# First and last turns of a graph-attention pipeline listed step by step, weights loaded in 21 transfers

## The chip, the core and the metric

The kernel runs on one core of a Trainium2 chip. A core has five engines with queues of their own: TensorE (matrix products, results into PSUM), VectorE, ScalarE, GpSimd and SyncE, which here only issues DMAs. Each engine works through its own queue in order and waits on semaphores for the others; 16 DMA engines move the data. The metric is the device time in microseconds of one execution; several executions give a median.

## The reference

There are 64 graphs of 256 nodes with 512 features, and two layers. All of it is float32.

```python
# layer 0, per graph
deg = sum(adj, -1);  agg = adj @ x / max(deg, 1e-6)
x = layernorm(x + relu(concat([x, agg], 2) @ W.T))
# layer 1, per graph: 8 heads of 64
q, k, v = x @ Wq.T + bq, x @ Wk.T + bk, x @ Wv.T + bv
scores = (q @ k.T) * 64 ** -0.5 * (adj + adj)
ctx = softmax(scores) @ v
out = layernorm(x + ctx @ Wo.T + bo)
```

## The kernel before

One graph goes through a chain of steps. A step is a small function, kept in a table by its name and called with a graph's number; the instructions it issues go into the queues of whatever engines they need. The names:

- `Dzx`, `Dza`, `Dx`, `Dadj` load x and the adjacency from HBM on SyncE's queue, in four DMAs each (`Dzx`, `Dza` in an order that VectorE's 32x32 block transposes `xT0`, `xT1`, `aT` turn into transposed tiles). `deg` makes the reciprocal degrees.
- `L1` to `L7` are layer 0's weight products, `AY0`, `AY1` the neighbour sums, `AYa`, `AYb`, `AYp`, `AYn` the joining, the statistics (VectorE), factors (GpSimd) and application (ScalarE) of the first norm, for each half of the rows.
- `Dway` stores the normalized rows to HBM, `Dz1` loads them in the order for the transpose `x1T`, and `Drest` loads them again for the residual, to which `bo` adds the bias row on GpSimd (line 496).
- `Q1` to `Q7` are the q and k projections together, `V1` to `V7` the v projection.
- `Sa` to `Sd` are the scores of four pairs of heads, and for each pair: `m` the mask and `M` the negated maximum (VectorE), `e` and `f` the exponentials (ScalarE), `r` the reciprocal, `n` the scaling (ScalarE), `T` a block transpose (VectorE), `Dw` a store to HBM and `Ds` its load as the transposed matrix.
- `C0a`, `C0b`, `C1a`, `C1b` are the context products, `c0`, `c1` ScalarE's copies of them out of PSUM, `O1` to `O7` the output projection, `lb`, `lp`, `ln` the last norm, `Dout` the store.

Each of the four projections (L, Q, V, O) is one level of a Strassen-Winograd scheme: seven products of half-size blocks in place of eight (line 307). The products need sums of blocks of the weights (`T1` to `T4`, made once) and of the tokens (`xS1` to `xS4`, `yS`, `cS`, on GpSimd, line 288). Products that share a PSUM bank accumulate in it; between them a bank's content is taken out by a `k` step (`Lk1`: a copy) or a `j` step (`Lj3`: an addition to what is there), so that `L6`, say, waits for `Lk1`.

The order of the work is written out by hand: `PLAN` is one turn of a software pipeline, and `name+n` means that in turn i the step is run for graph i+n. The loop at the end runs turns from -6 to B+5; a step for a graph that doesn't exist, or one already run, is left out. The same text thus serves the first and last turns.

The weights are loaded ahead of the turns, by `first_weights` and `more_loads`: a block at a time, and, except for wo, in four groups of 32 partitions, so 16 DMAs of 64 KB for each 512 x 512 matrix (w0 has two of these), 4 for wo. W0's lower half, wq and the four bias loads go on ScalarE's queue, the others on SyncE's. Tiles have a slot per block sum; T3 starts as the loaded block B12, which `sum_blocks` overwrites. `later_weights` (scalings and sums of wq and wk on VectorE, of wv on GpSimd) and `last_weights` (bv times wo into the bias row, sums of wo) run in the middle of the turns where graph 0 gets to `V2` and to `bo`.

Of the kernel before, what the change touches and what calls it, by code (L numbers as in the profile page):

```python
# [18 lines left out]

PLAN = """  # L20
# [37 lines left out]
    Q2+1 Qk4+1 AYp1+2 ln1-1 Qj2+1  # L58
"""
# [3 lines left out]
def kernel(  # L63
# [88 lines left out]
    B11, B21, B22, T1, T2, T3, T4 = range(7)  # L152
    w0 = const.tile([P, 7, 2, 2, G], F32, name="w0")
    wqk = const.tile([P, 7, 2, 2, G], F32, name="wqk")
    wv = const.tile([P, 7, 2, G], F32, name="wv")
    wo = const.tile([P, 7, 2, G], F32, name="wo")

    def load_blocks(queue, dst, dram, swapped=False, natural=False):

        for blk, kh, nh in ((B11, 0, 0), (T3, 0, 1), (B21, 1, 0), (B22, 1, 1)):  # L160
            nh ^= swapped
            cols = dram[:, nh * G : (nh + 1) * G]
            if natural:
                rows = cols.rearrange("(c p) o -> p c o", p=P)
                queue.dma_start(out=dst(slice(None), blk), in_=rows[:, 2 * kh : 2 * kh + 2])
                continue
            rows = cols.rearrange("(a c l) o -> a l c o", a=A, c=FC)
            for a, part in groups():
                queue.dma_start(out=dst(part, blk), in_=rows[a, :, 2 * kh : 2 * kh + 2])

    def sum_blocks(engine, w):
        for dst, a, b in ((T1, T3, B11), (T2, B22, T1), (T3, B22, T3), (T4, B21, T2)):
            engine.tensor_tensor(w[:, dst], w[:, a], w[:, b], ALU.subtract)  # L173

# [4 lines left out]
    def first_weights():  # L179
        load_blocks(nc.scalar, lambda p, k: w0[p, k, :, 1], w0t[F:])  # L180
        load_blocks(nc.sync, lambda p, k: w0[p, k, :, 0], w0t[:F])
        load_blocks(nc.scalar, lambda p, k: wqk[p, k, :, 0], wqt, swapped=True)
        nc.scalar.dma_start(out=bqk[:, 0], in_=bq)
        nc.scalar.dma_start(out=bqk[:, 1], in_=bk)
        nc.scalar.dma_start(out=bvT, in_=bv.rearrange("o (c p) -> p (o c)", p=P))
        nc.scalar.dma_start(out=bo_sb, in_=bo.to_broadcast([P, F]))
        for name in ("xT0", "xT1", "xS1", "xS2", "xS4", "xS3"):
            run(name, 0)
        sum_blocks(nc.vector, w0.rearrange("p k c m o -> p k (c m o)"))

    def more_loads():
        load_blocks(nc.sync, lambda p, k: wqk[p, k, :, 1], wkt, swapped=True)
        load_blocks(nc.sync, lambda p, k: wv[p, k], wvt)
        load_blocks(nc.sync, lambda p, k: wo[p, k], wot, natural=True)

    def later_weights():
        nc.vector.tensor_scalar(bqk[:, 0], bqk[:, 0], QSCALE, None, ALU.mult)
        for k in (B11, T3, B21, B22):
            nc.vector.tensor_scalar(wqk[:, k, :, 0], wqk[:, k, :, 0], QSCALE, None, ALU.mult)
        sum_blocks(nc.vector, wqk.rearrange("p k c m o -> p k (c m o)"))  # L200
        sum_blocks(nc.gpsimd, wv.rearrange("p k c o -> p k (c o)"))

    def last_weights():

        bv_all = tile_of("bv_all", 0, [P, NT, F], tag="h1")[:, 0].rearrange("p (c q) -> p c q", c=FC)
        nc.vector.tensor_copy(bv_all, bvT.unsqueeze(2).to_broadcast([P, FC, P]))
        ps = bank("p_bv", 0)
        for n, blocks in enumerate(((B11, B21), (T3, B22))):
            for c in range(FC):
                nc.tensor.matmul(  # L210
                    ps[:, n * G : (n + 1) * G],
                    lhsT=bv_all[:, c],
                    rhs=wo[:, blocks[c // 2], c % 2],
                    start=(c == 0),
                    stop=(c == FC - 1),
                )
        nc.vector.tensor_tensor(bo_sb, ps, bo_sb, ALU.add)
        sum_blocks(nc.gpsimd, wo.rearrange("p k c o -> p k (c o)"))
# [125 lines left out]
    def right_weights(left, w, width):  # L344
        def multiply(k, b, ps, first):
            for c in range(2):
                nc.tensor.matmul(  # L347
                    ps[:, :width],
                    lhsT=left(k, b, c),
                    rhs=w[:, WEIGHTS[k], c],  # L350
# [19 lines left out]
    def multiply_q(k, b, ps, first):  # L370
        for m in range(2):
            for j in range(2):
                for c in range(2):
                    nc.tensor.matmul(  # L374
                        ps.rearrange("p (m j q) -> p m j q", m=2, j=2)[:, m, j],
                        lhsT=wqk[:, WEIGHTS[k], c, m, j * P : (j + 1) * P],
# [264 lines left out]

    plan = [(name[:-2], int(name[-2:])) for name in PLAN.split()]
    done = set()

    def run(name, b):
        if 0 <= b < B and (name, b) not in done:
            done.add((name, b))
            steps[name](b)

    with tc.manual_schedule():  # L650
        run("Dzx", 0)
        first_weights()
        run("Dza", 0)
        run("Dadj", 0)
        run("Dx", 0)
        run("Dadj", 1)
        run("Dadj", 2)
        run("Dzx", 1)
        more_loads()
        for i in range(-6, B + 6):  # L660
            for name, ahead in plan:
                if name == "V2" and i + ahead == 0:
                    later_weights()
                if name == "bo" and i + ahead == 0:
                    last_weights()
                run(name, i + ahead)
# [36 lines left out]
```

## Time and profile before

| | |
|---|---|
| median of 3 runs | 3129.31 us (3128.94 to 3130.68) |
| profiled execution, its own time | 3130.71 us |
| its span, first to last instruction | 3128.9 us |
| TensorE busy | 3062.6 us, 98% of the span |
| VectorE, ScalarE, GpSimd busy | 67%, 55%, 31% |
| DMA | 513.35 MB, 164 GB/s on average |
| mean granted clock of TensorE | 0.992 |

The rows of a timeline read: start, duration (us), engine, line and operation, tiles out<-in, shapes, count, and in brackets how long the engine had been idle and what released it. PE is TensorE's matmuls, PEld its weight loads, DVE VectorE, ACT ScalarE, POOL GpSimd, SPq and ACTq the DMA issues of SyncE and ScalarE. A float32 product shows twice the matmuls that the code has[...]. A count such as "x4" merges equal neighbours.

### The profile page before, as it was taken

The page shows a single profiled execution, that of the slowest core. Times are in us where ns is not written, and L with a number is a line of the kernel's source. Part 1 is how long each engine was busy: PE and PEld are TensorE (multiplying, and loading weights), DVE is VectorE, ACT ScalarE, POOL GpSimd, SP SyncE. Part 2 cuts the span into 40 slices and gives each one's busy share as a digit, 9 for nine tenths or more (in the row PEclk, how much of TensorE's full clock was granted, in tenths as well). Part 3 has the DMA queues.
Part 4 walks back from the last instruction along what each step waited for, and adds up shares of the span by engine and source line. Part 5 has one row for each costly group of instructions (what it writes and reads, how often), then busy time and mean ns, then how long its engine had stood idle before and what let it go on. Part 6 is the DMA issues. An engine that isn't in the chain of part 4 may idle for free. (4 is left out here: it accounts for less than half of the span.)

```text
span 3128.9 us, 51253 instructions
## 1 busy us (share of the span) xinstructions
PE 3062.6 (98%) x17168; PEld 2265.9 (72%) x17168; DVE 2082.1 (67%) x3599; ACT 1712.2 (55%) x4993; POOL 974.2 (31%) x1677
## 2 busy tenths in 40 slices
PE   5999999999999999999999999999999999999996
PEld 2776777777777777777767777777777777777674
DVE  4666666666766766666666666667667666666664
ACT  1555556555555555555555565555555555555654
POOL 2233323323233233233333233232332332333332
PEclk8999999999999999999999999999999999999998
DMA  6565655656656656656666567566566566566555
GB/s 148 125 165 159 182 160 157 185 154 160 182 156 161 182 153 171 173 151 182 165 159 182 154 163 186 155 159 181 157 161 182 152 172 173 151 182 165 159 155 141
DMA packets 498183, 513.35 MB, mean 164 GB/s; under 512 B 114816, under 2 KB 399488, under 8 KB 497920
## 3 DMA queue, kind: packets, MB, share of 16 engines
q1 hardware_dynamic: 494400, 507.70, 60.5%
q8 instruction: 137, 2.24, 0.3%
q10 hardware_dynamic: 3520, 2.37, 0.3%
q14 instruction: 126, 1.03, 0.1%
HBM read 308.55 MB, written 201.33 MB: 163 GB/s over the span
## 5 line engine op out<-in xcount | busy, mean ns | idle before, releaser
L390 ACT ACTIVATE qk<-Qa,bqk 128x128 f32<-128x128 f32 x768 | 218.6, 367 | 241.2 <-PE Qa L374 241.2
L363 ACT COPY oy<-La 128x512 f32<-128x512 f32 x192 | 112.3, 585 | 433.2 <-PE La L347 433.1
L428 POOL TENSOR_SCALAR mv<-mv 128x1 f32<-128x1 f32 x256 | 55.7, 217 | 935.1 <-DVE mv L423 919.4
L405 ACT COPY v<-Va 128x256 f32<-128x256 f32 x192 | 70.1, 365 | 365.3 <-PE Va L347 365.3
L347 PE MATMUL Lc<-w,xS 128*128 128x512 f32 x512 | 249.8, 611 | 14.5 <-DVE w L173 14.5
L374 PEld LDWEIGHTS Qa<-x1T,wqk 128*128 128x128 f32 x2048 | 248.8, 192 | 6.6
L374 PEld LDWEIGHTS Qa<-yS,wqk 128*128 128x128 f32 x2048 | 248.8, 192 | 6.6
L288 POOL TENSOR_TENSOR cS<-cT 128x256 f32<-128x256 f32 x128 | 93.2, 729 | 509.2 <-ACT cT L616 509.2
L374 PE MATMUL Qc<-yS,wqk 128*128 128x128 f32 x2048 | 249.6, 275 | 0.0
L374 PE MATMUL Qa<-x1T,wqk 128*128 128x128 f32 x2048 | 249.3, 275 | 0.0
L374 PE MATMUL Qa<-yS,wqk 128*128 128x128 f32 x2048 | 249.3, 275 | 0.0
L347 PE MATMUL La<-w,xS 128*128 128x512 f32 x512 | 243.3, 598 | 5.4 <-POOL xS L288 3.0
L347 PE MATMUL La<-w,xT 128*128 128x512 f32 x512 | 241.6, 594 | 0.8 <-DVE oy L328 0.8
L374 PEld LDWEIGHTS Qc<-yS,wqk 128*128 128x128 f32 x2048 | 239.0, 192 | 0.0
L442 PE MATMUL AY<-oy,aT 128*128 128x512 f32 x512 | 233.0, 598 | 4.6 <-DVE oy L328 4.6
L415 DVE TENSOR_TENSOR h<-Oa,rest 128x256 f32<-128x256 f32 x192 | 81.5, 425 | 220.3 <-PE Oa L347 200.7
L328 DVE TENSOR_TENSOR oy<-Lc,oy 128x512 f32<-128x512 f32 x64 | 44.2, 691 | 276.0 <-PE Lc L347 271.0
L288 POOL TENSOR_TENSOR yS<-x1T 128x256 f32<-128x256 f32 x128 | 93.3, 729 | 350.2 <-DVE x1T L482 350.2
L347 PEld LDWEIGHTS Lc<-w,xS 128*128 128x128 f32 x512 | 93.2, 192 | 132.3 <-issue 108.8
L288 POOL TENSOR_TENSOR xS<-xT 128x256 f32<-128x256 f32 x128 | 93.4, 730 | 299.1 <-DVE xT L253 299.1
L454 DVE SCALAR_TENSOR_TENSOR oy<-AY,deg,oy 128x512 f32<-128x512 f32 x128 | 94.9, 741 | 135.7 <-PE AY L442 135.7
L546 ACT ACTIVATE sa<-sa,nmaxa 128x256 f32<-128x256 f32 x256 | 127.0, 497 | 99.8 <-DVE nmaxa L540 99.8
(119 smaller groups left out, 7274.4 us busy)
## 6 DMA issues: line engine op xcount, KB each, us to landing
zx<-in_x_dram SPq DMA_DIRECT2D x256, 128.0 KB, 3.6
x<-in_x_dram SPq DMA_DIRECT2D x256, 128.0 KB, 3.4
way<-x SPq DMA_DIRECT2D x64, 512.0 KB, 3.2
z<-way SPq DMA_DIRECT2D x256, 128.0 KB, 3.0
wsa<-sa SPq DMA_DIRECT2D x64, 512.0 KB, 2.6
wsb<-sb SPq DMA_DIRECT2D x64, 512.0 KB, 3.0
sTa<-wsa SPq DMA_DIRECT2D x256, 128.0 KB, 3.6
wsc<-sc SPq DMA_DIRECT2D x64, 512.0 KB, 2.7
```

The source lines that it names most:

```text
L288: nc.gpsimd.tensor_tensor(part_of(s, b, [P, 4, 2, P])[:, k], left(b), right(b), op)
L328: nc.vector.tensor_tensor(dst, ps.rearrange(shape, **sizes), dst, ALU.add)
L347: nc.tensor.matmul(ps[:, :width], lhsT=left(k, b, c), rhs=w[:, WEIGHTS[k], c], start=first and c == 0, stop=True, skip_group_check=True,)
L363: nc.scalar.copy(part_l(b, t, n), ps.rearrange("p (m o) -> p m o", m=2))
L374: nc.tensor.matmul(ps.rearrange("p (m j q) -> p m j q", m=2, j=2)[:, m, j], lhsT=wqk[:, WEIGHTS[k], c, m, j * P : (j + 1) * P], rhs=left_y ...
L390: nc.scalar.activation(part_q(b, t, n)[:, m, j], ps.rearrange("p (m j q) -> p m j q", m=2, j=2)[:, m, j], AF.Identity, bias=bqk[:, m, c : ...
L405: nc.scalar.copy(part_v(b, t, n), ps[:, :G])
L415: nc.vector.tensor_tensor(part_o(b, t, n), ps[:, :G], rest, ALU.add)
L428: nc.gpsimd.tensor_scalar(mv[:, 1:2], mv[:, 1:2], LN_EPS, None, ALU.add)
L442: nc.tensor.matmul(ps, lhsT=held["aT", b][:, j, t], rhs=held["oy", b][:, 1, j], start=(j == 0), stop=(j == NT - 1),)
L454: nc.vector.scalar_tensor_tensor(h, held[f"AY{t}", b], rdeg, h, ALU.mult, ALU.add)
L546: nc.scalar.activation(rows(b)[:, r], rows(b)[:, r], AF.Exp, bias=of("nmax", b)[:, r : r + 1], accum_out=of("total", b)[:, r : r + 1],)
```

## The change

Two texts are added beside `PLAN`: `START` lists, step by step with the graph's number, everything that belongs to the turns before turn 3, and `END` everything from turn 60 on (there `name:n` means graph B-n). The loop runs turns 3 to 59 with `PLAN`, which is as it was. The loads, scalings and sums of weights are steps of their own and stand in `START`: `W0`, `Wq`, `Wv`, `Wo`, `Wb` (loads), `WqS` (scaling of wq and bq), `W0s1` to `Wos4` (sums), `bv1` to `bv3` (the bias row).

A matrix is loaded with its rows whole, in 4 DMAs of 256 KB (wo: one of 1 MB), into a tile whose blocks are views; the sums T1, T2 and T4 have a tile of their own, and T3 overwrites the view of the block B12, as before it overwrote that block's slot. In `W0`, the lower half goes on ScalarE's queue and the upper on SyncE's; all other weights and the biases go on SyncE's. The scaling of wq and bq is on ScalarE, in two instructions; the sums of w0 and wq are on VectorE, those of wv and wo on GpSimd. The right operand of L's products is now two runs of 256 columns, one from each half of w0, where it was 512 columns in a row.

```diff
+FIRST_TURN = 3
+LAST_TURNS = 4
+START = """
+    Dzx:0 W0:0 xT1:0 xT0:0 xS1:0 xS3:0 Dx:0 xS2:0 Dza:0 xS4:0 Dadj:0 Dzx:1 L1:0 W0s1:0 W0s2:0 Dadj:1
+    L2:0 Lk1:0 W0s3:0 Wo:0 L6:0 W0s4:0 deg:0 L5:0 Lk6:0 aT:0 Wb:0 L7:0 Lk5:0 L3:0 Lj7:0 Dza:1 L4:0 Wq:0
+    Lj3:0 Lj2:0 Lk4:0 xT1:1 AY1:0 xT0:1 xS1:1 AY0:0 xS3:1 AYa1:0 L5:1 AYb1:0 AYa0:0 AYp1:0 L1:1 Dzx:2
+    xS2:1 AYn1:0 AYb0:0 L2:1 bv1:0 AYp0:0 aT:1 xS4:1 bv2:0 AYn0:0 Lk1:1 Dway:0 Wv:0 Lk5:1 Lj2:1 L6:1
+    Wos1:0 Lk6:1 WqS:0 L7:1 Dz1:0 L3:1 Lj7:1 Wqs1:0 Dx:1 L4:1 Lj3:1 Dadj:2 Wvs1:0 Wqs2:0 Lk4:1 Wos2:0
+    Dza:2 AY1:1 x1T:0 AY0:1 xT1:2 yS1:0 deg:1 yS2:0 Q1:0 Wqs4:0 Wvs3:0 AYa1:1 Wvs2:0 V1:0 Qk1:0 Q5:0
...
+    Vk5:0 xS4:2 AYn1:1 Vj7:0 deg:2 Dway:1 V3:0 Dza:3 Qk4:0 V4:0 Vj3:0 Vk4:0 Sa:0 Sb:0 ma:0 Sc:0 Dz1:1
...
+    Lj3:3 fa:1 L4:3 Md:1 Dz1:2 ra:1 Lk4:3 Sb:1 Dadj:4 na:1 Sc:1 mb:1 C0a:0 Lj2:3 fd:1 C1a:0 Mb:1 C1b:0
...
+    Vk4:3 Oj3:1 Drest:2 lb0:1 Dsd:2 lb1:1 V3:3 Qk4:3 V2:3 lp1:1 AYn0:4 Vj2:3 xS1:5 Vj3:3 ln1:1 lp0:1
+    xS3:5
+"""
 PLAN = """
...
+END = """
+    Dza:2 Sb:4 xS2:2 AYn1:3 Sa:4 xS4:2 mb:4 Dway:3 Sc:4 Mb:4 Sd:4 C1a:5 mc:4 fb:4 C0a:5 ma:4 ln0:6 C1b:5
...
+    Ta:2 yS3:1 ec:2 Q7:1 Qj3:1 Dwa:2 ed:2 rc:2 O6:3 Qj7:1 nc:2 Ok6:3 Sb:1 rd:2 mb:1 O7:3 nd:2 Sa:1 Dsa:2
+    Mb:1 O5:3 Tc:2 Q4:1 fb:1 Ok5:3 Dwc:2 Oj7:3 ma:1 Qk4:1 O4:3 Ma:1 eb:1 Q2:1 Td:2 ea:1 O2:3 Ok4:3 Dwd:2
+    Qj2:1 fa:1 C0a:2 Drest:2 Dsc:2 rb:1 Sc:1 nb:1 ra:1 Sd:1 Dsb:2 mc:1 O3:3 na:1 lb1:3 Dsd:2 Mc:1 lp1:3
+    Oj3:3 fc:1 Oj2:3 V1:1 lb0:3 ec:1 C1a:2 Ta:1 lp0:3 C0b:2 bo:2 ln1:3 md:1 Dwa:1 V5:1 ln0:3 rc:1 Md:1
+    C1b:2 nc:1 Dout:3 ed:1 Tc:1 fd:1 Tb:1 Dwc:1 Dsa:1 c0:2 rd:1 c1:2 Dwb:1 nd:1 O1:2 cS1:2 O2:2 cS2:2
+    Ok1:2 cS3:2 O6:2 Vk1:1 Td:1 Vk5:1 cS4:2 O5:2 Oj2:2 Dwd:1 V6:1 Ok6:2 Dsc:1 Ok5:2 O7:2 Vk6:1 V7:1
+    Dsb:1 Oj7:2 O4:2 O3:2 Ok4:2 lb1:2 Drest:1 V3:1 Dsd:1 Vj7:1 lp1:2 Oj3:2 V4:1 lb0:2 V2:1 Vk4:1 lp0:2
+    ln1:2 Vj2:1 Vj3:1 ln0:2 C0a:1 Dout:2 C1a:1 C0b:1 bo:1 C1b:1 c0:1 c1:1 O2:1 cS1:1 O1:1 cS2:1 O5:1
+    cS4:1 Ok1:1 O6:1 cS3:1 Ok5:1 O3:1 Ok6:1 Oj2:1 O7:1 Oj3:1 Oj7:1 lb0:1 O4:1 lp0:1 Ok4:1 lb1:1 ln0:1
+    lp1:1 ln1:1 Dout:1
+"""
...
-    B11, B21, B22, T1, T2, T3, T4 = range(7)
...
+    B11, B12, B21, B22, T1, T2, T4 = range(7)
+    T3 = B12
...
+    def weights(name, engine, parts, flip=0):
+        raw = const.tile([P, parts, FC, 2, G], F32, name=name)
+        sums = const.tile([P, 3, parts, 2, G], F32, name=f"{name}_sums")
+
+        def block(k):
+            if k >= T1:
+                return sums[:, k - T1]
+            return raw[:, :, k // 2 * 2 : k // 2 * 2 + 2, k % 2 ^ flip]
+
+        def put(n, dst, a, b):
+            steps[f"{name}s{n}"] = lambda _: engine.tensor_tensor(block(dst), block(a), block(b), ALU.subtract)
+
+        for n, blocks in enumerate(((T1, B12, B11), (T2, B22, T1), (T3, B22, B12), (T4, B21, T2))):
+            put(n + 1, *blocks)
+        return raw, block
...
+    def load_weights(queue, raw, part, dram):
+        rows = dram.rearrange("(a c l) (n o) -> a l c n o", a=A, c=FC, n=2)
+        for a, p in groups():
+            queue.dma_start(out=raw[p, part], in_=rows[a])
+
+    @step("W0")
+    def _(_):
+        load_weights(nc.scalar, w0_raw, 1, w0t[F:])
+        load_weights(nc.sync, w0_raw, 0, w0t[:F])
+
+    @step("Wq")
+    def _(_):
+        load_weights(nc.sync, wqk_raw, 0, wqt)
+        load_weights(nc.sync, wqk_raw, 1, wkt)
...
+    @step("WqS")
+    def _(_):
+        nc.scalar.mul(bqk[:, 0], bqk[:, 0], QSCALE)
+        nc.scalar.mul(wqk_raw[:, 0], wqk_raw[:, 0], QSCALE)
...
             for c in range(2):
                 nc.tensor.matmul(
-                    ps[:, :width],
+                    ps[:, :width].rearrange("p (m o) -> p m o", o=G),
                     lhsT=left(k, b, c),
-                    rhs=w[:, WEIGHTS[k], c],
+                    rhs=w(WEIGHTS[k])[:, :, c],
...
     with tc.manual_schedule():
-        run("Dzx", 0)
-        first_weights()
...
-        for i in range(-6, B + 6):
-            for name, ahead in plan:
...
+        for name, b in listed(START):
+            run(name, b)
+        for i in range(FIRST_TURN, B - LAST_TURNS):
+            for name, ahead in turn:
                 run(name, i + ahead)
+        for name, b in listed(END):
+            run(name, B - b)
```

## The prediction

> **What bounds the kernel now.** I read the busy times first, then the slices with the granted clock. "PE busy 98%" is not proof by itself, because matmul ends are modelled; the rows of the slices show where the other 2% sit: in the first slice and the last, where the clock is also low.
>
> ```profile
> PE 3062.6 (98%) x17168; PEld 2265.9 (72%) x17168; DVE 2082.1 (67%) x3599; ACT 1712.2 (55%) x4993; POOL 974.2 (31%) x1677
> ...
> PE   5999999999999999999999999999999999999996
> ...
> PEclk8999999999999999999999999999999999999998
> ```
>
> Then I cut the span at turns. Step Sa (first scores of a turn) starts on TensorE at 95.80 for graph 0, at 232.92 for graph 3 and at 2940.22 for graph 60. The stretches (columns: TensorE, weight loads, VectorE, ScalarE, GpSimd busy, granted clock, DMA share, GB/s):
>
> ```profile
> 0.00:95.80 95.80, 60.45 (x212) 35.17 (x212) 38.89 (x57) 14.71 (x33) 21.44 (x37) 0.88 0.49 121
> 95.80:232.90 137.10, 136.66 (x761) 101.20 (x760) 93.73 (x159) 75.66 (x229) 40.94 (x67) 1.00 0.64 164
> 232.90:2940.30 2707.40, 2707.40 (x15279) 2011.23 (x15278) 1839.27 (x3192) 1524.72 (x4447) 857.56 (x1483) 1.00 0.62 167
> 2940.30:3073.50 133.20, 130.98 (x798) 101.55 (x800) 88.87 (x152) 77.50 (x231) 39.51 (x68) 1.00 0.62 165
> 3073.50:3109.00 35.50, 19.74 (x98) 11.85 (x94) 16.94 (x29) 17.50 (x53) 7.38 (x12) 0.71 0.56 155
> 3109.00:3128.90 19.90, 7.37 (x28) 4.91 (x28) 4.42 (x11) 2.15 (x4) 7.35 (x12) 0.80 0.11 27
> ```
>
> The middle is 57 turns of 47.50 us, TensorE without a hole. From start-to-start times at full clock one graph holds: L 7 products of 1.715, AY 3.43, Q 7 of 1.787, V and O 14 of 0.862, S 3.45, C 3.45; 46.9 us in all, so 0.6 us of small gaps per turn. What is loose lies outside: up to Sa of graph 0 TensorE has 49.4 us of such work and takes 95.8 (46 lost); from Sa of graph 60 it has 147.9 and takes 188.7 (41 lost).
>
> The timeline names the holes.
>
> ```profile
> 14.53 3.75 PE L347 MATMUL Lc<-w,xS 128*128 128x512 f32 x4 [14.53 <-DVE w L173]
> ...
> 48.40 0.41 SPq L469 DMA_DIRECT2D way<-x  x1
> ...
> 55.30 2.33 SPq L475 DMA_DIRECT2D z<-way  x4
> ...
> 62.86 2.05 PE L347 MATMUL Vb<-wv,x1T 128*128 128x256 f32 x4 [10.06 <-issue]
> ...
> 63.50 4.63 DVE L199 TENSOR_SCALAR wqk<-wqk 128x512 f32<-128x512 f32 x4
> ...
> 68.06 5.82 DVE L173 TENSOR_TENSOR wqk<-wqk 128x1024 f32<-128x1024 f32 x4
> ...
> 74.53 6.31 PE L442 MATMUL AY<-oy,aT 128*128 128x512 f32 x8 [4.57 <-DVE oy L328]
> ```
>
> Graph 0's layer-0 rows are ready at 45, but their store stands in SP's queue behind 36 weight loads, and x1T comes only at 61.5: 10 us without a matmul. Then 10.5 us of scalings and sums of wqk block VectorE, and AY of graph 1 waits for its joins. At the other end, the last attention's transfers come home late and GpSimd's bias add stands ahead of a sum that O needs:
>
> ```profile
> 3099.66 2.14 SPq L584 DMA_DIRECT2D sTd<-wsd  x4
> ...
> 3104.07 1.98 PE L600 MATMUL pc<-sTc,v 128*64 128x256 f32 x8 [8.64 <-DMA sTc<-wsc]
> ...
> 3111.88 2.48 POOL L496 TENSOR_TENSOR rest<-rest,bo_sb 128x512 f32<-128x512 f32 x2
> ...
> 3113.66 1.13 PE L347 MATMUL Oa<-wo,cS 128*128 128x256 f32 x4 [1.35 <-DVE h L415]
> ```
>
> **The change: the start.** The list holds 184.2 us of TensorE work up to Sa:3.
>
> *First matmul.* It now needs zx (0.5 MB) and all of w0 (2 MB). The first 10 us moved 1.69 MB, of which some 2.5 pass before a byte moves (an estimate; a zx load lands 3.6 after its issue): 225 GB/s. 2.5 MB from 2.7 end at 13.8; first product at 14.2 (before: 14.53, after a sum that is no longer first). The row weighed against a rule: the Trainium skill (DMA: Bandwidth & Descriptors, Specifications) gives a core about 358 GB/s of HBM; 2.5 MB would be there at 10 and the total 4 us lower. No window here passes 255 GB/s, so I keep the row.
>
> *Clock.* After the idle start, matmuls went at half pace from 14.5 to 18.5 (0.86 us per 512 columns against 0.43): 2 us lost, once.
>
> *Up to Sa:0.* L and AY of two graphs, the bias product (3.43, pulled forward), Q and V but one product: 52.0 us. The copy Lk1 no longer waits behind ScalarE's DMA issues (36 there before, 4 now; it ran at 23.5 and held L6 by 2.4 us). AY follows L4 at once, so its last eviction shows: 0.7 twice.
>
> *Is x1T:0 in time?* On SP, 49 issues stand ahead of Dway:0; by the rows (four of zx 3.4, sixteen of w 7.5 to 10.4, four of za 3.2, of x 1.8) these end at about 32. Dzx:2 waits besides for xT of graph 1, which waits for L4:0 at 28. AY:0 ends at 34; two pairs of 0.74 + 0.69, stats 0.86, factors 1.3, apply 0.8 bring Dway:0 to 39.5. Ahead of it in the ring are 8.26 MB; at 225 GB/s they end at 39.4. Store 3.2, then Dz1 behind Wv's 1 MB: landed at 49.5, x1T at 51, where TensorE wants it at 52. I put 1 us. Here a rule speaks against the change: by the same page (Queues, rings and completion order) an engine takes descriptors in ring order, and now Wq and the biases leave ScalarE's ring for SP's. Had the ring only the 177 GB/s of 10 to 50 us before, Dway would start at 49, x1T come at 60, and the sum be 9.5 us higher with the clock lost again. That rate was one of 64 KB issues, 0.47 to 0.65 us each (100 to 136 GB/s per queue); Wq and Wo are now 256 KB and 1 MB an issue, so I keep 225.
>
> *Sums and scaling.* WqS goes to ScalarE: 256 columns from SBUF take it 0.50 us, 512 take 0.81, so 2048 some 3, where ScalarE has 4 of 8.6 us taken; without that cover it would delay Lk copies by 3. The W0, Wq sums (1.22 each) fit VectorE, loaded 5 to 8 us per 8.6 of TensorE; Wv, Wo sums on GpSimd (1.44 each) likewise. Nothing for them.
>
> So Sa:0 at 14.2 + 2 + 52 + 1.4 + 1 + 1 (small gaps) = 71.6, say 72. To Sa:3 the rest, 132.2, with gaps: before it took 137.1 for 134.8, so 2.3, and 1 for a new order: 135.5. Context of graph 0 stands 50 us after its scores and isn't late. **Start 207.5** (232.9 before). Floor: no wait at all, 202.7. Ceiling: 218, with the slow ring.
>
> **The middle.** Same order, same engines. The one difference is L's moving operand: two runs of 256 in place of 512 in a row, 28 matmuls a graph. S and C read theirs in runs of 32 and still go 8 in 0.86 us, V's rate per column with two at a time; I take nothing. 57 × 47.5 = **2707.3**.
>
> **The end.** 147.9 us of work; S of graph 63 ends at 122.9 of it, plus 2.5 lag (1.6 of usual gaps, 0.9 because Qj2:1 on VectorE follows a queue of T, M and Oj). I walked VectorE and ScalarE through the list from there, each in order: Mc:1 at 3 after it, Ta:1 at 6, Md:1 at 8, Tc:1 at 10, Tb:1 at 11.5, rd:1, then Td:1 at 15, and Dwd:1. On ScalarE c0:2 and c1:2 stand behind ec, fc, the two ln, nc, ed and fd of graph 63, and are done 12 after S, while TensorE reaches O1:2 5 after it: a stall of 6 to 7, with half clock afterwards (3.4 us of idle before 3088.97 brought 0.52 us a matmul). Over VectorE the load is 28.7 us where TensorE has 26.1: it, not TensorE, sets the pace there. SP then issues Dsc, Dsb, Drest, Dsd after Dwd (2.1 each, 0.5): sTd issued by 23, landed at 27 (before: 5 us after its issue). TensorE's own rest (10.3 us from O1:2, some at half clock) is done at about the same time. C1b:1 ends at 154.5.
>
> After it 20.4 us remained before. Now bo (2.5 on GpSimd) is ahead of C1b:1, and O no longer waits for it: copies 1.1, sums and seven products with their evictions to 8, stats 0.9, factors 1.4, apply 0.8, out 4.4 (from the end of the applies at 3124.54 to 3128.9): 16. Plus 1 for what the walk misses. **End 171.5** (188.7 before). Floor 159.5: no stall, then 10 after O's products. Ceiling: 188.7.
>
> **Sum.** 207.5 + 2707.3 + 171.5 = 3086.3 of span, against 3128.9. The profiled execution's own time is 3130.71 and the median of the runs 3129.31, 0.4 over that span; so **3087 us**, 1.4% faster.
>
> **Rivals.** (a) *The ring is slow*: Dz1:0 comes at 58 or later, TensorE stands 7 to 10 us before Q1:0 and restarts at half clock. For it: in the old run the store took 6.9 us behind wo, not 3.2. Against: fewer bytes ahead. 3096 to 3100. (b) *The end gives nothing*: the copies behind the exponentials, and an overfull VectorE, cost what is won; end 185 to 189: 3102. For it: the load count above; against: bo and Sa, Sb of graph 63 are earlier, and nothing there got slower. (c) *Both ends at their floors*: 3070. Against it: every list above has queues with less than 1 us of slack. (d) *Slower*: L's two-run operand. If each of the 28 matmuls a graph in the middle costs 26 ns or more beyond 428, 57 turns give back the 42 us; at 40 ns the time is 3151. Against: the S and C rows. (e) *Nothing happens*: a new hole as long as the old at both ends, 3129.
>
> **How the numbers follow.** Forecast 0.60 (its own range 3076 to 3096), (a) 0.15, (b) 0.12, (c) 0.08, (d) 0.03, (e) 0.02. The range 3070 to 3104 leaves out (d), (e), the top of (b) and the lowest of (c): less than 2 in 10. A measurement here tells 0.2% (6 us) from no change; (d) gives slower 0.03, (e) same 0.02, the rest faster 0.95.
>
> **What would show it.** Right: first matmul 14 to 15 as La from xT; one long run of matmuls up to Sa:0 at 70 to 75; Sa:3 at 205 to 212; 47.5 a turn, 512-column matmuls still 0.43 apart; C1b of graph 63 some 16 before the end. Wrong in the start if a wait for x1T or DMA of several us comes before Q; wrong in the middle if the turn isn't 47.5; wrong at the end if Sc of graph 63 is later than 127 after turn 60's start, or TensorE waits elsewhere than at O1:2 and C of graph 63.

## Result, and the profile after

The changed kernel takes 3092.72 us (median of four runs, 3090.42 to 3093.68), where the kernel before, run beside it, took 3129.99 (3128.94 to 3131.17): a ratio of 0.988 (95% interval 0.9863 to 0.9897), 1.2% faster. The forecast was 3087, with a range of 3070 to 3104. The profiled execution took 3093.68 us, its span is 3091.9.

First the busy times, and the rows of the slices for TensorE and its granted clock, of the kernel after:

```profile
PE 3057.1 (99%) x17168; PEld 2262.9 (73%) x17168; DVE 2079.8 (67%) x3594; ACT 1713.5 (55%) x4995; POOL 979.9 (32%) x1677
...
PE   7999999999999999999999999999999999999997
...
PEclk9999999999999999999999999999999999999998
```

The work is the same: as many matmuls as before, and busy times within 0.6% on every engine. Only the first and the last slice of TensorE's row differ, from 5 and 6 to 7 and 7. The stretches, cut as before at the first scores of graph 0, of graph 3 and of turn 60, and the last one at the end of graph 63's scores and of its context products (columns: TensorE, weight loads, VectorE, ScalarE, GpSimd busy, granted clock, DMA share, GB/s):

```profile
0.00:71.84 71.84, 55.15 (x224) 34.28 (x224) 38.65 (x59) 16.60 (x34) 27.26 (x39) 1.00 0.88 182
71.84:206.19 134.35, 134.35 (x750) 98.44 (x749) 90.45 (x151) 74.76 (x228) 37.85 (x62) 1.00 0.58 155
206.19:2913.50 2707.31, 2707.31 (x15278) 2013.22 (x15277) 1838.57 (x3193) 1524.49 (x4448) 858.78 (x1486) 1.00 0.62 167
2913.50:3043.10 129.60, 128.30 (x778) 94.98 (x777) 91.00 (x150) 80.99 (x247) 39.14 (x62) 1.00 0.56 153
3043.10:3074.40 31.30, 23.69 (x116) 15.75 (x116) 16.59 (x31) 14.41 (x38) 11.96 (x20) 0.89 0.95 243
3074.40:3091.90 17.50, 8.32 (x28) 6.20 (x28) 4.54 (x11) 2.21 (x3) 4.94 (x10) 0.72 0.12 31
```

Against the forecast:

| stretch | before | forecast | after |
|---|---|---|---|
| to first scores of graph 0 | 95.8 | 72 | 71.8 |
| from there to first scores of graph 3 | 137.1 | 135.5 | 134.4 |
| turns 3 to 59 | 2707.4 | 2707.3 | 2707.3 |
| to the end of graph 63's scores | 133.2 | 125.4 | 129.6 |
| to the end of its context products | 35.5 | 29.1 | 31.3 |
| the rest | 19.9 | 17 | 17.5 |

The start gave 26.7 us where 25.4 were foreseen, and the middle nothing, as foreseen. The end gave 10.3 where 17.2 were foreseen. In a second profile of the same kernel (the first experiment below) the last three stretches together took 175.9 in place of 178.4, so that 4 to 7 us of the end are what the forecast has wrong.

The timeline of the kernel after, at the places where the one of before had its holes:

```profile
15.86 3.75 PE L435 MATMUL La<-W,xT 128*128 128x512 f32 x4 [15.86 <-DMA W<-in_w0t_dram]
...
39.25 0.39 SPq L557 DMA_DIRECT2D way<-x  x1
44.30 1.79 SPq L563 DMA_DIRECT2D z<-way  x4
44.85 1.90 ACT L282 ACTIVATE Wq<-Wq 128x2048 f32<-128x2048 f32 x1
...
51.85 1.25 DVE L570 STREAM_TRANSPOSE x1T<-z 128x1024 f32<-128x1024 f32 x1 [1.30 <-DMA z<-way]
53.67 1.95 PE L462 MATMUL Qa<-x1T,Wq 128*128 128x128 f32 x16
...
3019.09 2.05 PE L462 MATMUL Qa<-x1T,Wq 128*128 128x128 f32 x16 [1.19 <-DVE x1T L570]
...
3049.38 1.98 PE L688 MATMUL pc<-sTc,v 128*64 128x256 f32 x8 [4.36 <-DVE sd L618]
...
3073.29 1.08 PE L688 MATMUL pc<-sTd,v 128*64 128x256 f32 x8 [2.28 <-DMA sTd<-wsd]
```

TensorE starts 1.3 us later than before, at half pace (four matmuls in 3.75 us; 1.88 is the usual), and then has no wait above 0.7 us up to the first scores: graph 0's rows are stored at 39.25 where it was 48.40, x1T starts at 51.85, and `Q1:0` begins at 53.67 with no wait in brackets, where the old run stood 10.06. What is left are three waits in the end: 1.19 us for x1T of graph 63, 4.36 before a context product of graph 62, 2.28 before the last one of graph 63. The name "sd" in the middle row is the last semaphore event before the start; the matrix that the product reads is sTc, whose loads were issued from 3040.7 on and landed 6.8 us later, as the view of this tile shows:

```profile
L672 SPq DMA_DIRECT2D sTc<-wsc x4: 422/455/777, 3040.7 to 3042.5; - x4
...
DMA to landing us min/median/max: 6.7/6.8/7.0
```

The last of the four, issued at 3042.5, was thus there at about 3049.3, where the product begins. It was a DMA that TensorE waited for.

### The profile page after: what moved, and what is told of

The parts are those of the page before. It is cut to its first block, busy times and chain, and to the rows that moved or that the text cites. A ratio compares the mean times of both kernels' runs of the same rounds, so it can differ in the third digit from the quotient of the medians.

```text
span 3091.9 us, 51161 instructions
## 1 busy us (share of the span) xinstructions
PE 3057.1 (99%) x17168; PEld 2262.9 (73%) x17168; DVE 2079.8 (67%) x3594; ACT 1713.5 (55%) x4995; POOL 979.9 (32%) x1677
## 3 DMA queue, kind: packets, MB, share of 16 engines
q10 hardware_dynamic: 576, 1.05, 0.2%
## 4 chain that ended last, share of the span: by engine, by line
PE 97%; DMA 2%; DVE 1%; POOL 0%; SPq 0%; issue 0%; ACT 0%; POOLq 0%; DVEq 0%
PE Qa L462 15%; PE La L435 14%; PE Lc L435 7%; PE pc L688 7%; PE Qc L462 7%; PE Oa L435 7%; PE AY L530 7%; PE Va L435 7%; PE Qb L462 4%; PE Oc L435 4%; PE Vc L435 4%; PE Lb L435 4%; PE sca L605 2%; PE scb L605 2%; PE scc L605 2%; PE Ob L435 2%
## 5 line engine op out<-in xcount | busy, mean ns | idle before, releaser
L584 POOL TENSOR_TENSOR rest<-rest,bo_sb 128x512 f32<-128x512 f32 x128 | 159.6, 1269 | 29.3 <-DMA rest<-way 29.3
L530 PEld LDWEIGHTS AY<-oy,aT 128*128 128x128 f32 x512 | 96.9, 190 | 96.7 <-issue 91.9
L517 POOL TENSOR_TENSOR mv<-mv,neg_half 128x1 f32<-128x1 f32 x256 | 144.3, 564 | 21.3
L435 PE MATMUL La<-W,xT 128*128 128x512 f32 x256 | 122.6, 602 | 15.9 <-DMA W<-in_w0t_dram 15.9
L634 ACT ACTIVATE sb<-sb,nmaxb 128x256 f32<-128x256 f32 x256 | 128.8, 511 | 3.6 <-DVE nmaxb L628 3.6
L462 PEld LDWEIGHTS Qa<-x1T,Wq 128*128 128x128 f32 x1024 | 124.4, 192 | 6.5 <-DVE x1T L570 1.8
L634 ACT ACTIVATE sd<-sd,nmaxd 128x256 f32<-128x256 f32 x256 | 127.2, 501 | 1.7 <-DVE nmaxd L628 1.7
L634 ACT ACTIVATE sc<-sc,nmaxc 128x256 f32<-128x256 f32 x256 | 127.3, 501 | 1.4 <-DVE nmaxc L628 1.4
L462 PEld LDWEIGHTS Qa<-x1T,Wq_sums 128*128 128x128 f32 x1024 | 124.4, 192 | 3.9 <-issue 0.8
L462 PEld LDWEIGHTS Qa<-yS,Wq 128*128 128x128 f32 x1024 | 124.2, 192 | 3.6 <-issue 0.5
```

The source lines that it names most:

```text
L435: nc.tensor.matmul(ps[:, :width].rearrange("p (m o) -> p m o", o=G), lhsT=left(k, b, c), rhs=w(WEIGHTS[k])[:, :, c], start=first and c == ...
L462: nc.tensor.matmul(ps.rearrange("p (m j q) -> p m j q", m=2, j=2)[:, m, j], lhsT=wqk(WEIGHTS[k])[:, m, c, j * P : (j + 1) * P], rhs=left_y ...
L517: nc.gpsimd.tensor_tensor(mv[:, 1:2], mv[:, 1:2], neg_half, ALU.pow)
L530: nc.tensor.matmul(ps, lhsT=held["aT", b][:, j, t], rhs=held["oy", b][:, 1, j], start=(j == 0), stop=(j == NT - 1),)
L584: nc.gpsimd.tensor_tensor(rest, rest, bo_sb, ALU.add)
L634: nc.scalar.activation(rows(b)[:, r], rows(b)[:, r], AF.Exp, bias=of("nmax", b)[:, r : r + 1], accum_out=of("total", b)[:, r : r + 1],)
```

## The experiments

The theory: start and end are two independent gains; the start's has two causes, the order of the steps and the number of loads; the end falls short because the list splits the products up and because DMAs of the last graphs come late. The rivals: the start's gain is the loads' alone; the end gives nothing; the end falls short through copies on ScalarE. All times are medians of four or more runs, and ratios are against runs of the kernel before on the same chip (3129.62, 3131.63 and 3131.35 us in the three sets).

### The changed kernel once more

No edit.

> The changed kernel again, beside the three that follow: 3092.7, within 2.

3093.41 us, ratio 0.9879 (0.9864 to 0.9894). Its profiled execution took 3090.71 with a span of 3088.9: turn 60's first scores at 2912.99, the last stretch 175.9. The wait before graph 62's sTc product is 2.67 here, followed by one of 1.23 for sTb, and the last is 2.12. So one profile's end is known only to some 2.5 us, and the waits for DMAs are what varies: sTc landed 5.0 after its issue here, 6.8 above.

### The old text for the last turns

```diff
-        for i in range(FIRST_TURN, B - LAST_TURNS):
+        for i in range(FIRST_TURN, B + 6):
             for name, ahead in turn:
                 run(name, i + ahead)
-        for name, b in listed(END):
-            run(name, B - b)
```

> START as listed, then PLAN's turns to the very end, as the old kernel had them. In the trace of the changed kernel the stretch up to Sa of graph 3 fell from 232.9 to 206.2 (26.7 us) and the stretch from turn 60 on from 188.7 to 178.4 (10.3). My theory: the two are independent, so this kernel takes 3092.7 + 10.3 = 3103, and its last stretch is 188.7 again. Rival: the new last stretch begins from another state (what START leaves in the queues shapes the turns), then this kernel differs from 3103 by more than 3 us.

3104.25 us, ratio 0.9918 (0.9903 to 0.9933). Graph 3's first scores stand at 206.69, turn 60's at 2914.00, and from there it takes 188.2, the 188.7 of before. `END` is worth some 11 us; the rival that it gives nothing falls.

### The old text and the old loads for the first turns

The kernel before, with `END` from turn 60 on.

```diff
-        for i in range(-6, B + 6):
+        for i in range(-6, B - 4):
...
+        for word in END.split():
+            name, b = word.split(":")
+            run(name, B - int(b))
```

> The old start with its 84 loads and the old layout of the weights, turns to 59, then END. My theory: 3130.0 - 10.3 = 3119.7, Sa of graph 3 at 232.9, a turn 47.50, last stretch 178.4. Rival (END's gain hangs on the new layout of the weights or on START): more than 3 us away from it.

3118.27 us, ratio 0.996 (0.9945 to 0.9974). Graph 3's first scores at 234.16, the last stretch 174.8, which is 3.6 and 1.1 below the two profiles of the changed kernel; the waits for x1T of graph 63 and for the last sTd are 0.38 and 1.21 in it. Against the 3129.62 of the same set, the last turns alone are worth 11.4 us and the first alone (the kernel above) 25.4; both in one kernel 37.3, by the two medians of the result. The two gains add up.

### 84 loads in the new order

Every matrix loaded in its quarters, as before, into the new tiles, everything else as changed.

```diff
-        for a, p in groups():
-            queue.dma_start(out=raw[p, part], in_=rows[a])
+        for kh, n in ((0, 0), (0, 1), (1, 0), (1, 1)):
+            for a, p in groups():
+                queue.dma_start(
+                    out=raw[p, part, 2 * kh : 2 * kh + 2, n], in_=rows[a, :, 2 * kh : 2 * kh + 2, n]
+                )
```

> START and END as in the changed kernel, but every matrix is loaded block by block in 64 KB DMAs (wo in four), 84 loads, in the places where START has the 21. My theory (the number of issues on SP decides when graph 0's rows can be stored): 12 + 24 + 3 more issues stand ahead of Dway:0, at 0.47 to 0.65 us each 18 to 25 us, so the store is issued at 52 to 60 in place of 39.3, x1T of graph 0 comes at 62 to 72 in place of 51.9, TensorE stands 10 us or more before Q1:0 and the kernel takes 3103 to 3115. Rival (the order alone made the start's gain, the loads are hidden): 3093, within 3.

3104.24 us, ratio 0.9917 (0.9901 to 0.9934). The timeline of this kernel:

```profile
10.36 3.75 PE L442 MATMUL La<-W,xT 128*128 128x512 f32 x4 [10.36 <-DMA W<-in_w0t_dram]
...
48.08 0.40 SPq L564 DMA_DIRECT2D way<-x  x1
...
61.87 1.25 DVE L577 STREAM_TRANSPOSE x1T<-z 128x1024 f32<-128x1024 f32 x1 [14.60 <-DMA z<-way]
63.17 3.78 PE L469 MATMUL Qa<-x1T,Wq 128*128 128x128 f32 x16 [13.27 <-DVE x1T L577]
```

The first product comes 5.5 us earlier, since it needs only a quarter of each half of w0. But graph 0's rows are ready at 35.3 (the end of their application on ScalarE), while SyncE, which issues one load after the other until then, gets to their store at 48.08, not 39.25, and TensorE stands 13.27 us for x1T: the hole of the kernel before, with the new order of the steps around it. Fewer loads are worth something not because TensorE gets its first weights sooner (it gets them later) but because SyncE's queue is empty when graph 0's rows are ready.

### 21 loads in the old order

The new tiles and loads, all issued ahead of the turns as before; the turns from -6 on with `PLAN`; scaling of wq back on VectorE, and the sums back where graph 0 gets to `V2` and `bo`.

```diff
+HEAD = "Dzx:0 W0:0 xT0:0 xT1:0 xS1:0 xS2:0 xS4:0 xS3:0 W0s1:0 W0s2:0 W0s3:0 W0s4:0 Dza:0 Dadj:0 Dx:0 Dadj:1 Dadj:2 Dzx:1 Wq:0 Wb:0 Wv:0 Wo:0"
...
-        nc.scalar.mul(wqk_raw[:, 0], wqk_raw[:, 0], QSCALE)
+        nc.vector.tensor_scalar(wqk_raw[:, 0], wqk_raw[:, 0], QSCALE, None, ALU.mult)
...
-        for name, b in listed(START):
+        for name, b in listed(HEAD):
             run(name, b)
-        for i in range(FIRST_TURN, B - LAST_TURNS):
+        for i in range(-6, B - LAST_TURNS):
             for name, ahead in turn:
+                if i + ahead == 0 and name == "V2":
+                    for step_of_weights in "WqS Wqs1 Wqs2 Wqs3 Wqs4 Wvs1 Wvs2 Wvs3 Wvs4".split():
+                        run(step_of_weights, 0)
...
```

> 21 loads, but the old order of the start: all weights loaded ahead of the turns (all but half of w0 on SP), wq's scaling and sums and wv's in one block where graph 0 gets to V2, the bias row and wo's sums at bo; then PLAN's turns from -6, and END. My theory: 53 issues in place of 84 bring the store of graph 0's rows from 48.4 to about 45, x1T from 61.5 to about 56, and the 10 us of scaling and sums on VectorE stay; so 4 to 8 of the 26.7 us of the start are the loads', Sa of graph 3 at 225 to 229, and the kernel takes 3111 to 3116. Rival (fewer loads are most of the start's gain): Sa of graph 3 below 215, 3102 or less.

3110.99 us, ratio 0.9936 (0.9921 to 0.9951). Graph 3's first scores stand at 223.9, so the larger loads brought 10.3 us where 4 to 8 were expected. The old wait behind the sums on VectorE is still there:

```profile
57.25 2.17 DVE L239 TENSOR_TENSOR Wq_sums<-Wq 128x1024 f32<-128x1024 f32 x1
...
66.69 5.18 PE L531 MATMUL AY<-oy,aT 128*128 128x512 f32 x8 [4.19 <-DVE oy L417]
```

With the three other kernels this makes a square of four. The first scores of graph 3 begin at:

| | 84 loads | 21 loads |
|---|---|---|
| old order | 234.2 | 223.9 |
| new order | 217.3 | 206.2 |

Either way the new order is worth 17 to 18 us and the larger loads 10 to 11. The two labels stand for more than they say: the corner with the old order and 84 loads is the start of the kernel before, which also has the old layout of the tiles and wq and the biases on ScalarE's queue, and the old order has the scaling on VectorE. The rival that the start is the loads' alone falls, and the two add up.

### The residual's load behind the context's

Here and below a list is shown only around the words that move. In `END`, for the last two graphs, `Drest` (the load of a graph's rows for the residual) is issued after the loads of the last attention matrix, not before.

```diff
     C0a:2
-    Drest:2
     Dsc:2
...
     Dsd:2
+    Drest:2
     Mc:1
...
     lb1:2
-    Drest:1
     V3:1 Dsd:1
+    Drest:1
     Vj7:1
```

> In END, Drest:2 and Drest:1 (the residual rows of graphs 62 and 61's successor, 512 KB each) are issued after Dsd of their graph in place of before the four Ds. In the changed kernel TensorE stands 4.4 us before the context product of pair c of graph 62, whose transposed matrix lands 6.7 us after its issue (3.5 is the median), and 2.3 us before the last pair of graph 63. My theory (transfers ahead in SP's ring delay the ones TensorE waits for, 512 KB at about 230 GB/s are 2.2 us each): both waits shrink by 2 us or more, time 3088 to 3091. Rival (VectorE's and ScalarE's queues set those moments): both waits stay within 0.5 us and the time stays at 3092.7.

3089.85 us, ratio 0.9868 (0.9853 to 0.9882); the last stretch is 174.7. Its timeline at the places of the two waits:

```profile
3047.51 1.08 PE L692 MATMUL pc<-sTc,v 128*64 128x256 f32 x8 [1.86 <-DVE stats L514]
...
3070.47 1.08 PE L692 MATMUL pc<-sTd,v 128*64 128x256 f32 x8 [0.39 <-DMA sTd<-wsd]
```

The last wait is gone but for 0.39. Its matrix lands 5.0 us after its issue, against 6.4 and 6.5 in the two profiles of the changed kernel. The wait before it is 1.21 to 2.28 us in all nine profiles that have `END` without this edit, and 0 to 0.39 in the three that have it. The wait of graph 62 can't be put down to this edit: with a following wait of 1.40 for sTb it is 3.3 us, where the repeated run above had 2.67 and 1.23. The total lies 3 us below that of the changed kernel, but the intervals of the two ratios overlap, so the gain is shown by the row of the last wait rather than by the time.

### The last graph's rows loaded earlier

In `END`, `Dz1` of graph 63 is issued right after `Dsb` of graph 61, ahead of `Dsd` and `Drest` of that graph.

```diff
     Dsb:3
+    Dz1:1
     ma:2
...
     Drest:3
-    Dz1:1
     md:2
```

> In END, Dz1:1 (layer-0 rows of the last graph, for the transpose) is issued right after Dsb:3 in place of after Dsd:3 and Drest:3. In the changed kernel TensorE waits 1.2 us for that transpose. My theory: the wait goes away, and nothing else gets late, 1 to 1.5 us less, 3091 to 3092. Rival: the 1.2 us come back as a wait for pair d of graph 61, or at the end, 3092.7.

3090.84 us, ratio 0.9875 (0.9859 to 0.9892). The wait for x1T is gone, and graph 63's first scores start at 3028.72 where it was 3030.54, with turn 60 starting at the same 2913.5: 1.8 us, of which the last stretch (174.1 us) keeps what the waits for sTc, sTb and sTd behind it (2.59, 1.36 and 1.62) leave. Here too the row shows the gain, and the time alone couldn't.

### One change of kind more in each turn

Full products are 128 rows by 128 columns of the array; the scores use 64 rows ("64*128" in the rows), the context 64 columns ("128*64"). `PLAN` runs the four steps of scores and the four of context in one group per turn. Here the last context product is moved behind one L product, in every turn.

```diff
-    C1b-1 Mb+0 Dz1+1 c1-1
-    L5+2 c0-1 mc+0 Dx+2 eb+0 cS3-1
+    Mb+0 Dz1+1
+    L5+2 C1b-1 c1-1 c0-1 mc+0 Dx+2 eb+0 cS3-1
```

> In PLAN, the context product C1b (8 matmuls of 64 columns) and its copy c1 move behind L5, so that one full-width product stands between two groups of half-width ones, in each of 57 turns; START and END as in the changed kernel. In END the scores and context products stand singly among full-width products, and each such change of kind seems to cost 0.1 us going in and 0.2 us coming out (score group after an O product 0.33 us without a weight load, next group 1.06 us after it where 0.86 is usual). My theory: a turn grows by 0.2 to 0.4 us, the kernel by 11 to 23 (3104 to 3116). Rival (a change of kind costs nothing, END loses time to its waits alone): a turn stays at 47.50 and the time within 3 us of 3092.7.

3111.89 us, ratio 0.9938 (0.9923 to 0.9952): 18 to 19 us more than the changed kernel over 57 turns. One turn of it in the timeline, from the first context product of a graph to that of the next:

```profile
1549.16 1.08 PE L688 MATMUL pc<-sTa,v 128*64 128x256 f32 x8
...
1597.01 1.08 PE L688 MATMUL pc<-sTa,v 128*64 128x256 f32 x8
...
1599.75 1.98 PE L435 MATMUL Lc<-W_sums,xS 128*128 128x512 f32 x4
1601.66 1.08 PE L688 MATMUL pc<-sTd,v 128*64 128x256 f32 x8
1602.68 1.98 PE L435 MATMUL La<-W,xT 128*128 128x512 f32 x4
```

A turn takes 47.85 in place of 47.50. The L product ahead of the moved one takes 1.91 to its successor's start where 1.715 is usual, the moved one 1.02 in place of 0.86: 0.2 on the way in and 0.15 on the way out, 0.35 for a group that stands alone. Neither of these rows has a wait in brackets.

### Wv's load behind graph 0's rows

```diff
     Dway:0
-    Wv:0
     Lk5:1
...
     Dz1:0
+    Wv:0
     L3:1
```

> In START, the load of wv (1 MB) is issued after Dz1:0 in place of before it. In the changed kernel graph 0's rows come home at 51.8, 7.5 us after the issue of their load at 44.3 (2.9 is the median), with wv in SP's ring between. By ring order they land 4 us earlier, x1T starts at 47 to 48.5, and TensorE, busy with AY until 53.7, gains nothing: 3092.7 within 2. Rival (the landing is late because many transfers share the engines, not by its place in the ring): x1T stays at 51 or later.

3092.26 us, ratio 0.9876 (0.9861 to 0.9891): no gain. But the ring did what was expected of it. The loads of graph 0's rows landed 2.9 us after their issue, where it was 5.9 in the changed kernel, so that the last of the four was there at about 48.5 and not at 51.7. x1T starts at 50.01 without a wait for a DMA, because VectorE's queue has a sum of wq ahead of it:

```profile
48.88 1.22 DVE L241 TENSOR_TENSOR Wq_sums<-Wq,Wq_sums 128x1024 f32<-128x1024 f32 x1
50.01 1.24 DVE L573 STREAM_TRANSPOSE x1T<-z 128x1024 f32<-128x1024 f32 x1
```

And TensorE now waits 1.45 us for a sum of graph 0's tokens, because the sums of wv, which wait for the later load, stand ahead of it on GpSimd. So the 1 MB ahead in the ring cost 3 us of the 4 expected; what the expectation left out are the queues of VectorE and GpSimd.

### The first weights in halves

W0 in 16 DMAs of 128 KB, the left columns of both halves first, so that the first product can start when half of it is there.

```diff
-        load_weights(nc.scalar, w0_raw, 1, w0t[F:])
-        load_weights(nc.sync, w0_raw, 0, w0t[:F])
+        for n in range(2):
+            for queue, part in ((nc.scalar, 1), (nc.sync, 0)):
+                rows = w0t[part * F : (part + 1) * F].rearrange("(a c l) (n o) -> a l c n o", a=A, c=FC, n=2)
+                for a, p in groups():
+                    queue.dma_start(out=w0_raw[p, part, :, n], in_=rows[a, :, :, n])
```

> W0 in sixteen transfers of 128 KB, the left column halves of both parts first; nothing else differs. With 84 loads the first product stood at 10.4 us in place of 15.9, because L1 and L2 need the left halves alone. My theory: the first product at 10.5 to 11.5, L and AY of two graphs done 4 to 5 us earlier, but the rows of graph 0 come home no earlier than 50 (the bytes ahead of their store are the same), so most of it turns into a wait before Q1:0: Sa of graph 0 at 69 to 72, time 3090 to 3092.7. Rival (the start is set by the first matmul): Sa of graph 0 at 67 or before, time 3088 or less.

3092.87 us, ratio 0.9876 (0.9861 to 0.9891): nothing. Its timeline:

```profile
13.45 2.90 PE L438 MATMUL La<-W,xT 128*128 128x512 f32 x3 [13.45 <-DMA W<-in_w0t_dram]
...
52.48 1.25 DVE L573 STREAM_TRANSPOSE x1T<-z 128x1024 f32<-128x1024 f32 x1 [4.01 <-DMA z<-way]
...
53.78 2.05 PE L465 MATMUL Qa<-x1T,Wq 128*128 128x128 f32 x16 [2.02 <-DVE x1T L573]
```

The first product is 2.4 us earlier, not the 4 to 5 expected, and all of it becomes a wait of 2.02 before `Q1:0`. x1T doesn't come sooner when the products before it do.

### The three together, and a larger version

The halves of W0, the late residual and the early rows in one kernel:

> The last one and the two edits in END together (residual rows after the transposed matrices; Dz1:1 early). Alone the two gave 2.9 and 1.9. My theory: they take away different waits, so 4 to 5 us, and the halves of W0 up to 2 more: 3086 to 3089. Rival (both hit the same chain of the last graph): 3089 to 3090.

3089.13 us, ratio 0.9865 (0.9848 to 0.9881); the last stretch is 173.4, against 176.5 with the halves alone. That is just above the 3086 to 3089 of the theory and within the 3089 to 3090 of the rival, so the time doesn't tell them apart. The rows do in part: the last wait and the one for x1T are gone, but 0.90 us come back as a wait for sTd of graph 61, those before graph 62's products stay at 2.32 and 1.11, and the halves still wait 2.45 before `Q1:0`. It is the best of all kernels run, 0.1% below the changed one, though the intervals overlap.

The last one adds to it (the diff is against that kernel; the lists are shown a few words at a time), in `START`, that the loads of wv and wo, the bias product and the sums of wv and wo come after graph 0's rows, and in `END`, that some score and context products are put side by side:

```diff
     W0s3:0
-    Wo:0
     L6:0
...
     xS4:1
-    bv2:0
     AYn0:0
...
     Dway:0
-    Wv:0
     Lk5:1
...
     L6:1
-    Wos1:0
     Lk6:1
...
     Dz1:0
+    Wv:0
     L3:1
...
     Dadj:2
-    Wvs1:0
     Wqs2:0 Lk4:1
-    Wos2:0
     Dza:2
+    Wo:0
     AY1:1
...
     yS2:0
+    Wvs1:0
     Q1:0
...
     Wvs2:0
-    V1:0
     Qk1:0
...
     AYa0:1
-    Vk1:0
     Wvs4:0 Q6:0
+    V1:0
     Qk5:0
+    Vk1:0
     Wqs3:0
...
     V7:0
-    bv3:0
     AYp1:1
...
     V4:0
+    bv2:0
     Vj3:0
+    bv3:0 Wos1:0 Wos2:0
     Vk4:0
...
     Vk6:2
-    C0a:3
     nb:2
...
     Vj2:2
+    V4:2 C0a:3
     C0b:3
...
     lp1:4
-    V4:2
     Vj3:2
...
     Sb:1
+    Sa:1
     rd:2
...
     nd:2
-    Sa:1
     Dsa:2
...
     ec:1
+    V5:1
     C1a:2
...
     Dwa:1
-    V5:1
     ln0:3
```

> As the last one, and in START the 2 MB of wv and wo (with the bias product and the sums of both) come after the load of graph 0's rows, so that 1 MB less stands ahead of their store and 1 MB less ahead of their load; in END Sa:1 moves next to Sb:1, V4:2 and C0a:3 next to C0b:3, V5:1 ahead of C1a:2, three changes of kind between half-width and full-width products fewer. My theory: x1T of graph 0 at 42 to 46, no wait of more than 1 us before Q1:0, Sa of graph 0 (which now has the bias product ahead of it as before) at 66 to 68, time 3080 to 3085. Rival (SP's issues, not the bytes, decide when the store goes out): x1T at 49 or later, time as the last one's within 1.5.

3090.7 us, ratio 0.9871 (0.9856 to 0.9886), a miss. x1T starts at 47.06, 4.8 us earlier than in the changed kernel, but TensorE then stands for a sum of wq on VectorE:

```profile
60.87 2.63 PE L472 MATMUL Qa<-yS,Wq 128*128 128x128 f32 x16 [2.97 <-DVE Wq L245]
```

That sum stands on VectorE behind a step which itself waited 3.33 us for x of graph 1, a load that now has wv's 1 MB ahead of it. Graph 0's first scores come at 74.94, 3 us later than in the changed kernel. In the end the grouping did what it was to do: between the first context product of graph 60 and the last scores of graph 63, start to start, the changes of kind cost 1.89 us at 14 places where the kernel with the three edits has 2.86 at 20, 0.32 for each of the three groups gone. Half of that went into a new wait of 0.46 for ScalarE's copy of a v product; the last stretch is 172.4.

## Why the prediction was right, and where not

**The start** (207.5 forecast, 206.2 measured) was right as a sum, and its terms cancel in part. Its first step came out 1.7 us late, and not by the rate. The stretch up to the first product, in the columns of the stretches above:

```profile
0.00:15.86 15.86, 0.00 (x0) 0.03 (x1) 1.37 (x3) 1.28 (x1) 3.10 (x9) 1.00 0.95 187
```

187 GB/s over 15.86 us are 2.97 MB; counted as the forecast counted, without the first 2.5 us, that is 222 GB/s, the 225 of the forecast. It was the bytes that were too few. The forecast wrote 0.5 and 2 MB for x and w0, which are 0.52 and 2.10 in the unit of the rate (the trace has 1.05 MB for the four loads of half of w0), so 2.62 MB in place of 2.5: half a us. And the other 0.35 MB are not what the product needs: the loads of x and of the adjacency, issued behind W0's on SyncE from 8.91 on, ran beside its last ones. (With the 358 GB/s that the prediction weighed and put aside, the step would have been off by 6 us. Its "no window passes 255" holds for stretches of 10 us in the trace of before; from 50 to 55 us that kernel moved 280 GB/s.)

The queue step was right up to the store: `Dway:0` was issued at 39.25 (39.5 forecast). From there it fell short by 2.2 us: the rows were back at about 51.7, not 49.5, mostly because the store landed 5.0 us after its issue, not 3.2. The same slip of units is in it: the 8.26 MB ahead in the ring are 8.66, and at 39.25 the core had moved 8.1 MB (207 GB/s), so half a MB was still to come. No wait for x1T appeared all the same, because TensorE, late by 1.7, was itself at work until 53.7. The 1.4 us for two evictions of AY didn't show either. So that the start came out within 1.3 us is in part luck: a late first product and late rows stand against waits that were put in and didn't come. The rule on the order in a ring, which stood against the change, holds here (1 MB put behind the rows' loads brings them 3 us sooner), but the ring was not slow: up to 44.3 the core moved 214 GB/s, not the 177 of the old start. Rival (a), the slow ring, asked for `Dz1:0` at 58 or later; it was issued at 44.30. WqS took 1.90 us on ScalarE where 3 were forecast, and delayed nothing.

That the start's gain comes from both the order and the loads was in the prediction as one chain (36 issues ahead of the store; sums that block VectorE); the square of four splits it: 17 to 18 and 10 to 11 us. The prediction costed neither alone.

**The middle** was right to 0.01 us. L's right operand in two runs of 256 costs nothing, and rival (d) falls: at the 26 ns a matmul from which it would have decided, the turns would be 0.73 us longer each.

**The end** is where the prediction failed: 171.5 forecast, 178.4 and 175.9 in two profiles. Both signs that it named for being wrong there are in the trace: `Sc` of graph 63 starts 127.6 us after turn 60 ("later than 127"), and TensorE waits at `C1a:2`, which is neither of the places it allowed. Two of its steps are wrong.

The first is the lag of 2.5 us until graph 63's scores are done ("1.6 of usual gaps, 0.9 because Qj2:1 follows a queue"); it was 6.7, with 129.6 in place of 125.4. The step took the gaps from `PLAN`'s turns, where there is one group of scores and context products per graph. `END` spreads them: up to graph 63's last scores the row of TensorE changes from full products to scores or context and back 24 times. That makes twelve groups of half-width products where 2.7 turns of `PLAN`, which is what 129.6 us are worth, would have 2.7. At the 0.35 us per group that the experiment with one group more in each turn measured (20 us in 57 turns), 9.3 groups more are 3.3 us. The rows agree: start to start, the products ahead of a change take 3.2 us beyond their own length, where 2.7 turns of `PLAN` (0.19 each) have 0.5, and those behind a change or within a group some 1.8, where `PLAN` has 1.0; 3.5 us are thus the price of the order itself. Another 1.2 is the wait for x1T of graph 63, which the edit with `Dz1` first took away. Against these stands the 0.9 for `Qj2:1`, which didn't show: TensorE has no wait before the last scores. What is left of the missing 4.2, about 0.4, is of the size of small gaps between q and k products (0.6), whose cause is open.

The second is the place of the stall. The prediction walked the lists to a wait of 6 to 7 us at `O1:2`, behind the copies c0 and c1 on ScalarE. ScalarE's rows of the kernel after:

```profile
3053.30 0.58 ACT L704 COPY cT<-pc 128x512 f32<-128x512 f32 x1
3056.21 0.59 ACT L704 COPY cT<-pc 128x512 f32<-128x512 f32 x1 [2.32 <-PE pc L688]
```

They end at 10.8 and 13.7 us after graph 63's scores, near the 12 that the walk gave for both; but the second waits for TensorE, not TensorE for it. TensorE had lost 4.36 us one step earlier, at `C1a:2`, where sTc of graph 62 wasn't there, and ran three groups at half pace after it (1.98 us where 1.08 is usual). The walk never asked when graph 62's loads land: it followed SyncE's queue for graph 63 alone. It named nearly the right size of loss for the wrong resource. The queue on ScalarE that it followed is real and comes next: in the kernel with the late residual, where the products of graph 62 are done earlier, TensorE waits 0.75 us at `O1:2` for a copy. Rival (b), which put a lost end down to those copies and to VectorE, is wrong as well: with `END` the last stretch is 10 to 14 us shorter. Rivals (c), both ends at their floors, and (e), no change, lie 23 us below and 36 above the measured time.

For the last pair, the walk had sTd landed 4 us after the last issue; it took 6.4, with `Drest` ahead of it, and the product waited 2.28. The experiment that puts `Drest` behind gets 5.0 and 0.39. The rest, from the last context product on, was forecast at 17 and took 17.5.

## What to carry to other kernels

A pipeline's turns written as one text are tuned for the steady state; what they cost at both ends is read from the span cut at turns, and bounds what a list for the ends can win (here 46 and 41 us of gaps, of which 27 and 10 to 13 came back). When such a list is costed, follow every queue for the last graphs but one too, and price the order itself: how often TensorE changes between full and half-width products. And where three limits lie within 2 us of each other (first weights, the rows' round trip, the weights' sums), easing one moves the wait to the next: of the edits of the start tried on top of the change none brought time.

## What the runs showed of the hardware

- **Changing the shape of the used array costs time.** 0.1 to 0.2 us on each side of a group of half-width float32 products, 0.35 per lone group, by the turn of 47.85 against 47.50. The Trainium skill (TensorEngine Tiling (Array Packing), Key Properties) says that a change of tiling mode drains the engine, with no price. The price is what is measured here; that a drain is the cause was not tried.
- **Sums on VectorE and GpSimd slow each other.** In the kernel after, a sum of wq on VectorE took 1.21 us with GpSimd idle, and one of the same size 2.16 when it began 0.18 us behind a GpSimd sum of wv. That one took the 1.27 that such a sum also takes at 39.02, where VectorE is idle for most of it; the next, which began while VectorE's was still running, took 2.25:

```profile
47.60 1.21 DVE L238 TENSOR_TENSOR Wq_sums<-Wq 128x1024 f32<-128x1024 f32 x1
...
54.66 1.27 POOL L238 TENSOR_TENSOR Wv<-Wv 128x512 f32<-128x512 f32 x1
54.84 2.16 DVE L238 TENSOR_TENSOR Wq_sums<-Wq,Wq_sums 128x1024 f32<-128x1024 f32 x1
55.88 2.25 POOL L238 TENSOR_TENSOR Wv_sums<-Wv,Wv_sums 128x512 f32<-128x512 f32 x1
```

  Each time the one that starts second is late by about what is left of the other (0.95 and 0.98 us, where 1.09 and 1.12 were left). The prediction took 1.22 and 1.44 for them; the difference was nearly covered (0.15 us of wait at 62.86).
- **Half pace follows gaps shorter than 3.4 us.** In the kernel after, the granted clock is 0.50 from 3049.4 to 3053.0, behind the wait of 4.36 us, and the products run at half pace there. Elsewhere such products came behind single waits of 2.31 (one change of kind more), 2.39 (the kernel before, at 24.22) and 2.45 us (the three edits together, at 53.75), and in the end behind waits of 2.32 and 1.11, of 2.67 and 1.23, and of 1.18, 1.48 and 0.78 with one or two products between them. None came behind a single 2.02, nor behind 1.86, 1.40, 0.34, 0.75 and 1.22 in a row (the late residual, granted clock 1.00 throughout). The Trainium skill (TensorE: Matmul & The Clock Gate, Part 1) puts the return to the slow clock after an idle window of about 3.4 us; none of the gaps in these lists is as long. Neither the longest gap nor their sum sorts all of these cases, so what does stays open.
- **One DMA's landing varies between executions of the same kernel:** 5.0 and 6.8 us after the issue for the same four loads of sTc, which is why one profile of the end settles no more than some 2.5 us.
